# The values of self-attention as 2 by 2 blocks: seven half-width products for eight

## Chip, cores, metric

The kernel runs on one core of one Trainium2 chip. Time is device time in microseconds (us) of one execution; a kernel is run several times and the median is quoted. A second source is the profile: one execution recorded by the hardware profiler, with every engine instruction's start and duration. TensorE is called PE in it (PEld its weight loads), VectorE DVE, ScalarE ACT, GpSimd POOL, and the queue that issues most DMAs SP.

## What is computed

One decoder layer in fp32, on 8 sequences of 112 tokens with 512 features: causal self-attention with 16 heads of 128, cross-attention to 8 contexts of 375 tokens, and a mixture-of-experts feed-forward. Only the values of the first part concern the change:

```python
k = jnp.einsum('ihd,bpd->biph', W_K, x)
q = jnp.einsum('ihd,bpd->biph', W_Q, x)
v = jnp.einsum('ihd,bpd->biph', W_V, x)
...
attn = jax.nn.softmax(masked / jnp.sqrt(jnp.float32(d_head)), axis=-1)
z = jnp.einsum('biqp,biph->biqh', attn, v)
```

For a group of four heads, `v` is a product of 896 tokens by 512 features with a weight of 512 by 512.

## The kernel before

**Tokens.** The 896 tokens stand in seven tiles of 128. Tile t holds the 112 tokens of sequence t + 1 and, in its last 16 rows, a seventh of sequence 0. `xn1` is the normalised input, features on the partitions in four chunks of 128 and the 896 tokens along the free axis; HALF is 448 tokens.

**Groups.** Self-attention runs over four groups of four heads (`for g in range(NG)`). In each, PE makes the queries and keys, then the values with the first scores, then the weighted sums and the output projection (`project_o`, L340 to L351). One pass over a group takes about 108 us.

**Queries and keys.** `pair_of_heads` (L249 to L282) already makes them as 2 by 2 blocks in Winograd's form, seven products for eight. Tokens are halved (first and last 448), features are halved, and the two heads of a pair are the two column halves. The token sums `xc` are made once, by `token_sums`; the weight sums are made by POOL for each pair (L253 to L256, in tiles `wc` with three buffers). Products go to PSUM; DVE (L273, L277, L280 to L282), ACT (L271, L275) and POOL (L278, L279) add them up.

**Values.** `value(t)` (L335 to L343) makes a plain product for one tile: four chunks of features, each a matmul of 128 stationary columns (tokens) and 512 moving columns, summed in one PSUM tile; ACT copies it to `vals[t + 1]`, and SP moves its last 16 rows to the tile `vals[0]` of sequence 0. The calls stand between the scores: `softmax(b)` for the sequences 1, 0, 2, 3, 4, one value tile after each, then two more tiles. A matmul in fp32 is two records of PE in the profile, so a group has 56 records for its values.

**Softmax.** `softmax(b)` gives PE four small matmuls (L191) and then a chain: DVE adds the mask (L199), takes the maximum (L206) and subtracts it (L207), ACT takes the exponential (L208), DVE sums (L210) and inverts (L211), POOL multiplies (L212). Sequences 5 to 7 are done after the values, between `turn` (transposes, L218, copied by ACT at L220) and `weighted` (L226, evicted by DVE at L233).

**Order and buffers.** A scheduler puts each engine's instructions into one fixed order when the program is built, and each engine works through its own in order, waiting on semaphores. PSUM tiles of the values come from the pool `mm`, four buffers that are used in turn: a product needs the eviction of the one four before it. The weights of the next group are loaded by SP during the group, as soon as a buffer is free.

Of the kernel before, what the change touches and what calls it, by code (L numbers as in the profile page):

```python
# [27 lines left out]
HALF = NT // 2  # L28
H, DH = 16, 128
GH = 4  # L30
# [46 lines left out]
def decoder_layer(  # L77
    ctx: ExitStack, tc: tile.TileContext, x, ctxT, wqk, wv_all, wo, wx, wgate, wsgu, wsd, wegu, wed_a, wed_b, consts, out
):
    nc = tc.nc  # L80
# [7 lines left out]
    mm = ctx.enter_context(tc.tile_pool(name="mm", bufs=4, space=PSUM))  # L88
# [67 lines left out]
    def ln_apply(mv, rs, t, xnT):  # L156
        xn = ln_normed(mv, rs, t)
        pt = psum(mm, "ln_t")
        for c in range(ND):
            nc.tensor.transpose(pt[:, c * P : (c + 1) * P], xn[:, c * P : (c + 1) * P], ident)  # L160
        nc.scalar.copy(xnT[:, :, t * P : (t + 1) * P], pt.rearrange("p (c s) -> p c s", c=ND))


    xn1 = xnpool.tile([P, ND, NT], F32, tag="xnT", name="xn1")
    mv1 = ln_begin("1")

    def norm1(lo, hi):
        for t in range(lo, hi):
            ln_stats(mv1, t)
        return [ln_rstd(mv1, lo, hi)] * (hi - lo)  # L170
# [6 lines left out]
    with ExitStack() as sa:  # L177
        wvpool = sa.enter_context(tc.tile_pool(name="weights_vo", bufs=2))
        xcp = sa.enter_context(tc.tile_pool(name="x_sums", bufs=1))
        wcp = sa.enter_context(tc.tile_pool(name="w_sums", bufs=3))  # L180
        up = sa.enter_context(tc.tile_pool(name="part", bufs=2))
        qkp = sa.enter_context(tc.tile_pool(name="qk", bufs=1))
        vp = sa.enter_context(tc.tile_pool(name="v", bufs=TT))
# [100 lines left out]
        for g in range(NG):  # L284
            if g == 0:

                wq, wk = (wpool.tile([P, 4, 512], F32, tag="w", name=f"w{i}_0") for i in range(2))
                for h in range(GH):
                    for i, w in enumerate((wq, wk)):
                        nc.sync.dma_start(out=w[:, h, :], in_=wqk[i, g][:, h, :])  # L290
            else:
                wq, wk = (load_w(wpool, wqk[i, g], f"w{i}_{g}") for i in range(2))
            wv = load_w(wvpool, wv_all[g], f"w2_{g}")
            wog = wvpool.tile([P, 4, 512], F32, tag="w", name=f"wo_{g}")
            load = nc.sync.dma_start(out=wog, in_=wo[g])
            if g == 0:
                first_weights = load.ins
                with tc.issue_after(first_weights):
                    nc.sync.dma_start(out=gw, in_=wgate)
                    nc.sync.dma_start(  # L300
                        out=slots.rearrange("(j p) d -> p j d", p=P),
                        in_=zeros[:, None, :].to_broadcast([P, NS, D]),
                    )
            qT = qkp.tile([P, GH, NT], F32, tag="qT", name="qT")
            kT = qkp.tile([P, GH, NT], F32, tag="kT", name="kT")
            zT = zp.tile([P, GH, NT], F32, tag="zT", name="zT")
            for h in range(0, GH, 2):
                for w, dst, pool in ((wq, qT, mm), (wk, kT, sc)):
                    if g == 0 and h == 0 and dst is qT:

                        for half in range(2):
                            cols = bass.ds(half * HALF, HALF)
                            for i in range(2):
                                ps = psum(mm, "qk")
                                for c in range(ND):
                                    nc.tensor.matmul(
                                        ps[:, :HALF],
                                        w[:, i, c * P : (c + 1) * P],
                                        xn1[:, c, cols],
                                        start=(c == 0),  # L320
                                        stop=(c == ND - 1),
                                    )
                                nc.scalar.copy(dst[:, i, cols], ps[:, :HALF])
                            if half == 0:
                                rs1 = norm1(4, TT)
                                for t in range(4, TT):
                                    ln_apply(mv1, rs1[t - 4], t, xn1)
                                token_sums()
                        continue
                    pair_of_heads(w, h, dst, pool)  # L330
            soft, turned, vals = {}, {}, {}
            vals[0] = v0p.tile([S, GH * DH], F32, tag="v0", name="v0")

            def value(t):

                ps = psum(mm, "v")
                for c in range(ND):
                    nc.tensor.matmul(  # L338
                        ps, xn1[:, c, t * P : (t + 1) * P], wv[:, c, :], start=(c == 0), stop=(c == ND - 1)
                    )  # L340
                vals[t + 1] = vp.tile([P, GH * DH], F32, tag="v", name="v")
                nc.scalar.copy(vals[t + 1], ps)
                nc.sync.dma_start(out=vals[0][t * SP : (t + 1) * SP, :], in_=vals[t + 1][S:, :])  # L343

            def project_o(t):
                ps = psum(mm, "o")
                for h in range(GH):
                    nc.tensor.matmul(  # L348
                        ps,
                        zT[:, h, t * P : (t + 1) * P],  # L350
                        wog[:, h, :],  # L351
                        start=(h == 0),
                        stop=(h == GH - 1),
                    )
                nc.vector.tensor_tensor(xs[t], ps, xs[t], ALU.add)  # L355
                if g == NG - 1:
                    ln_stats(mv2, t)


            q0 = vp.tile([P, GH, S], F32, tag="q0", name="q0", bufs=1)  # L360
            nc.gpsimd.tensor_copy(like_seq(q0, 0), seq(qT, 0))
            for i, b in enumerate((1, 0, 2, 3, 4)):
                soft[b] = softmax(b, qT, kT, q0)
                value(i)
            for i in (5, 6):
                value(i)
            for b in (1, 0):
                turned[b] = turn(soft.pop(b))
            for b in range(1, B):
                if b + 4 < B:  # L370
                    soft[b + 4] = softmax(b + 4, qT, kT, q0)
                if b + 1 < B:
                    turned[b + 1] = turn(soft.pop(b + 1))
                weighted(b, turned.pop(b), vals.pop(b), zT)
                if b == 2:
                    weighted(0, turned.pop(0), vals.pop(0), zT)
                elif b > 2:
                    project_o(b - 3)
            project_o(TT - 2)
            project_o(TT - 1)  # L380
# [8 lines left out]
    with ExitStack() as xa:  # L389
# [14 lines left out]
        values = [v1p.tile([MC, NM, XH, VW], F32, name=f"v1_{i}") for i in range(2)]  # L404
# [49 lines left out]
        wt = [stp.tile([P, 2, 512], F32, name=f"wt{i}") for i in range(2)]  # L454
# [24 lines left out]
        def product(x, w):  # L479
            ps = psum(mm, "kv")  # L480
            for c in range(2):
                nc.tensor.matmul(ps[:MC, :], x[:, c, :], w[:, c, :], start=(c == 0), stop=(c == 1))  # L482
            return ps[:MC, :]
# [244 lines left out]
    with ExitStack() as ff:  # L728
# [37 lines left out]
        part = rp.tile([P, NT], F32, name="part")  # L766
# [124 lines left out]
        rows = []  # L891
# [282 lines left out]
```

## Time and profile before

| | us |
|---|---|
| median of 5 runs | 1019.46 (1017.88 to 1021.17) |
| the profiled execution | 1021.62 |
| its span (first to last engine instruction) | 1019.8 |
| PE busy | 997.1, 98% of the span |
| DVE, ACT, POOL busy | 401.4, 277.1, 246.8 |
| granted PE clock, mean | 0.996 |
| values, matmuls of the four groups (L338) | 224 records |

A busy time counts each moment once, even where matmuls overlap in the pipeline. The chain of waits follows the end of the program back, at each step to what released it; its pieces add up to the time. A stage table gives each engine's busy time in a stretch of the span.

### The profile page before, as it was taken

Reading aid. Unit: us, or ns where it says so; the run is one execution under the profiler, and the core shown is the slowest. Engines: PE = TensorE matmul, PEld = TensorE weight load, DVE = VectorE, ACT = ScalarE, POOL = GpSimd, SP = SyncE. Lnnn points to the kernel's source line nnn. Section 1 sums busy time; section 2 is a strip of 40 time slices with the busy share of each in tenths; the row PEclk is TensorE's granted clock in tenths of the full one; section 3 lists DMA queues with packets and bytes.
Section 4 is the critical chain, followed back from the end, with each engine's and each line's share of the span. In section 5 each row is a group of like instructions: output and inputs, shape, how many; then the busy total and the mean of one; then the engine's idle time right before and its main releaser. Section 6 shows DMA issues by size and latency. Waiting matters only on the chain.

```text
span 1019.8 us, 14761 instructions
## 1 busy us (share of the span) xinstructions
PE 997.1 (98%) x5732; PEld 530.8 (52%) x5732; DVE 401.4 (39%) x769; ACT 277.1 (27%) x522; POOL 246.8 (24%) x269
## 2 busy tenths in 40 slices
PE   5999999999999999999999999999999999999998
PEld 3556555554556455645455555555565544444433
DVE  3345224442345225545432434343424333333315
ACT  2122011210022012214354555445543111112200
POOL 3241034112511122122533213330205500000023
PEclk9999999999999999999999999998999999999999
DMA  9421012101101111000000100000209838777665
GB/s 348 190 86 48 0 42 84 50 1 42 61 30 43 42 41 47 5 1 0 31 31 2 31 31 32 2 31 2 83 2 369 298 93 276 233 232 235 214 194 168
DMA packets 31093, 95.66 MB, mean 94 GB/s; under 512 B 3888, under 2 KB 5808, under 8 KB 27440
## 3 DMA queue, kind: packets, MB, share of 16 engines
q1 hardware_dynamic: 25968, 82.11, 23.7%
q0 software_dynamic: 2320, 7.63, 2.3%
q10 hardware_dynamic: 2736, 4.98, 1.7%
q8 instruction: 46, 0.75, 0.3%
q14 instruction: 23, 0.19, 0.1%
HBM read 78.85 MB, written 14.94 MB: 92 GB/s over the span
## 4 chain that ended last, share of the span: by engine, by line
PE 90%; DVE 4%; issue 3%; POOL 1%; DMA 1%; ACT 1%; SPq 0%; DVEq 0%; POOLq 0%; ACTq 0%
PE qk L261 15%; PE o L348 9%; PE v L338 9%; PE kv L482 9%; PE gu L744 5%; PE xs L577 5%; PE gate L980 4%; PE y L1002 4%; PE up L980 4%; PE pv L602 4%; PE ys L1028 3%; PE k L423 3%; PE xv L423 3%; PE z L226 2%; PE s L191 2%
## 5 line engine op out<-in xcount | busy, mean ns | idle before, releaser
L585 ACT ACTIVATE e<-xs 125x448 f32<-125x448 f32 x192 | 88.6, 545 | 73.3 <-PE xs L577 73.2
L338 PE MATMUL v<-w,xn 128*128 128x512 f32 x224 | 100.4, 594 | 0.0
L348 PE MATMUL o<-wo,zT 128*128 128x512 f32 x224 | 99.8, 594 | 0.0
L261 PE MATMUL qk<-xc,wc 128*128 128x448 f32 x180 | 70.1, 539 | 0.0
L348 PEld LDWEIGHTS o<-wo,zT 128*128 128x128 f32 x224 | 41.0, 190 | 44.1 <-issue 44.0
L338 PEld LDWEIGHTS v<-w,xn 128*128 128x128 f32 x224 | 40.7, 190 | 42.1 <-issue 41.1
L212 POOL TENSOR_TENSOR s<-s,sm 112x448 f32<-112x448 f32 x32 | 30.1, 942 | 128.7 <-DVE sm L211 112.4
L1013 POOL DMA_INDIRECT got<-routed,at x14 | 14.9, 1066 | 172.6 <-DMA routed<-y 168.5
L980 PE MATMUL gate<-wex,xT 128*64 x144 | 55.3, 466 | 0.5 <-ACT xT L945 0.5
L744 PE MATMUL gu<-xn,sw 128*128 128x448 f32 x144 | 55.5, 541 | 0.0
L980 PE MATMUL up<-wex,xT 128*64 x144 | 54.3, 459 | 0.0
L577 PE MATMUL xs<-qT,kT 32*125 32x224 f32 x768 | 51.6, 378 | 1.5 <-DVE qT L540 1.5
L261 PEld LDWEIGHTS qk<-xc,wc 128*128 128x128 f32 x180 | 34.2, 190 | 33.5 <-issue 32.3
L930 DVE COPY xn<-wex 128x704 f32 x60 | 31.2, 525 | 51.5 <-PE up L980 51.5
L577 PEld LDWEIGHTS xs<-qT,kT 32*125 32x125 f32 x768 | 33.8, 184 | 32.7 <-issue 28.7
L261 PE MATMUL qk<-xn,w 128*128 128x448 f32 x120 | 50.2, 539 | 0.0
L1002 PE MATMUL y<-wd,hT 128*64 128x512 f32 (+1 forms) x216 | 49.5, 593 | 0.6 <-ACT y L1006 0.6
L980 PE MATMUL gate<-xn,xT 128*64 128x352 f32 x120 | 45.9, 464 | 0.0
L980 PE MATMUL up<-xn,xT 128*64 128x352 f32 x120 | 45.3, 459 | 0.0
L355 DVE TENSOR_TENSOR x<-o,x 128x512 f32<-128x512 f32 x28 | 19.3, 690 | 62.2 <-PE o L348 62.2
L271 ACT COPY p<-qk 128x448 f32<-128x448 f32 x15 | 8.0, 532 | 126.7 <-PE qk L261 126.7
L208 ACT ACTIVATE s<-s 112x448 f32<-112x448 f32 x32 | 18.5, 577 | 84.2 <-DVE s L207 78.9
(211 smaller groups left out, 1672.9 us busy)
## 6 DMA issues: line engine op xcount, KB each, us to landing
wd<-in_wed_a SPq DMA_DIRECT2D x27, 512.0 KB, 3.7
wex<-in_wegu SPq DMA_DIRECT2D x8, 1408.0 KB, 19.3
wd<-in_wed_b SPq DMA_DIRECT2D x36, 192.0 KB, 4.4
w<-in_wqk SPq DMA_DIRECT2D x6, 1024.0 KB, 4.9
ctx<-in_ctxT SPq DMA_DIRECT2D x8, 750.0 KB, 8.8
slots<-zeros SPq DMA_DIRECT2D x1, 4608.0 KB
wd<-in_wed_a SPq DMA_DIRECT2D x18, 256.0 KB, 4.2
routed<-y SPq DMA_DIRECT2D x18, 256.0 KB, 3.3
```

Source lines behind the costliest of these rows:

```text
L261: nc.tensor.matmul(ps[:, :HALF], wt[:, c * P : (c + 1) * P], x[:, c, :], start=(c == 0), stop=(c == 1))
L338: nc.tensor.matmul(ps, xn1[:, c, t * P : (t + 1) * P], wv[:, c, :], start=(c == 0), stop=(c == ND - 1))
L348: nc.tensor.matmul(ps, zT[:, h, t * P : (t + 1) * P], wog[:, h, :], start=(h == 0), stop=(h == GH - 1),)
L423: nc.tensor.matmul(ps[:MC, :], ctxs[b][:, c, m * MC : (m + 1) * MC], w[:, c, :], start=(c == 0), stop=(c == ND - 1),)
L482: nc.tensor.matmul(ps[:MC, :], x[:, c, :], w[:, c, :], start=(c == 0), stop=(c == 1))
L577: nc.tensor.matmul(strips[j][:MC, ci * 2 * S : (ci + 1) * 2 * S], keys[b][rows, 2 * cp + ci, m * MC : (m + 1) * MC], queries[b][rows, 2 * ...
L585: last_exp[(b, cp, m)] = nc.scalar.activation(e[:, :, j, :, :].rearrange("p c e s -> p c (e s)"), strips[j][:MC, : 4 * S].rearrange("p (c ...
L602: nc.tensor.matmul(ps[VW * j : VW * (j + 1), g * S : (g + 1) * S], v[:, m, 16 * cp + h, :], es[m][:, h // 8, (h % 8) // 2, h % 2, :], star ...
L744: nc.tensor.matmul(ps[:, :HALF], w[:, c, i % 2, k, :], xn3[:, c, cols], start=(c == 0), stop=(c == ND - 1))
L930: nc.vector.tensor_copy(second(j, c), wex[:, bass.ds(moved[j], 1), c, :].rearrange("p o f -> p (o f)"))
L980: nc.tensor.matmul(gu[k][n, :FF], xT[:, c, n], w, start=(c == 0), stop=(c == ND - 1))
L1002: nc.tensor.matmul(ps[n, :], hT[:fn, i, n], w[i][:fn], start=(i == 0), stop=(i == len(FCH) - 1))
```

## The change

The values of a group are made in two parts.

`values_left()` makes the first 64 tokens of tile 0 and the last 64 tokens of tile 3 plainly. For each chunk of features, two matmuls with 64 stationary columns and 512 moving columns stand next to each other as column tiles of the array: one writes the PSUM rows 0 to 63, the other the rows 64 to 127 of the same PSUM tile. ACT copies the two halves to `vals[1]` and `vals[4]`.

`values()` makes the rest in three rounds of 2 by 2 blocks. In round i the low tokens are the 128 from token 64 + 128 i on (half of one tile and half of the next), and the high tokens are 448 later, which is exactly tile 4 + i. The columns are halved to 256 (`wide`). The token sums `xc` of the queries and keys are used again; four weight sums (128 x 512 elements each) are new and are made by POOL in two tiles of the pool behind `wc`. Each round has seven products of two matmuls with 256 moving columns, and each product its own PSUM tile from `mm`. They are combined by DVE (two additions to `u2` and `u3`, one to the high tile, and four of 64 rows, `low`, which write the rows of one half tile from PSUM rows of the other half), by ACT (two copies) and by POOL (two additions).

The generator yields after every product; after each of the five early `softmax` calls four products are taken, and the last one after them. `values_left()` stands ahead of the first softmax. The copies of the last 16 rows of each tile (`tail`) are issued at the end of each round.

```diff
-            def value(t):
-                ps = psum(mm, "v")
-                for c in range(ND):
-                    nc.tensor.matmul(
-                        ps, xn1[:, c, t * P : (t + 1) * P], wv[:, c, :], start=(c == 0), stop=(c == ND - 1)
-                    )
-                vals[t + 1] = vp.tile([P, GH * DH], F32, tag="v", name="v")
-                nc.scalar.copy(vals[t + 1], ps)
-                nc.sync.dma_start(out=vals[0][t * SP : (t + 1) * SP, :], in_=vals[t + 1][S:, :])
+            def values_left():
+                ps = psum(mm, "v")
+                n = P // 2
+                for c in range(ND):
+                    for rows, lo in ((slice(0, n), 0), (slice(n, P), HALF)):
+                        nc.tensor.matmul(
+                            ps[rows, :], xn1[:, c, lo : lo + n], wv[:, c, :], start=(c == 0), stop=(c == ND - 1)
+                        )
+                nc.scalar.copy(vals[1][:n, :], ps[:n, :])
+                nc.scalar.copy(vals[4][n:, :], ps[n:, :])
+            wide = D // 2
+            b11, b12 = wv[:, 0:2, :wide], wv[:, 0:2, wide:]
+            b21, b22 = wv[:, 2:4, :wide], wv[:, 2:4, wide:]
...
+            nc.gpsimd.tensor_tensor(wt[0], b12, b11, ALU.subtract)
+            nc.gpsimd.tensor_tensor(wt[1], b22, wt[0], ALU.subtract)
+            nc.gpsimd.tensor_tensor(wt[2], b22, b12, ALU.subtract)
+            nc.gpsimd.tensor_tensor(wt[3], b21, wt[1], ALU.subtract)
+            def values():
+                n = P // 2
+                for i in range(3):
+                    lo = bass.ds(n + i * P, P)
+                    hi = bass.ds(HALF + n + i * P, P)
+                    high = vals[5 + i]
+                    def product(x, cols, w):
+                        ps = psum(mm, "v")
+                        for c in range(2):
+                            nc.tensor.matmul(ps[:, :wide], x[:, c, cols], w[:, c, :], start=(c == 0), stop=(c == 1))
+                        return ps[:, :wide]
...
+                    def low(cols, a, b):
+                        nc.vector.tensor_tensor(vals[1 + i][n:, cols], a[:n], b[:n], ALU.add)
+                        nc.vector.tensor_tensor(vals[2 + i][:n, cols], a[n:], b[n:], ALU.add)
+                    p1 = part("p1")
+                    nc.scalar.copy(p1, product(xn1[:, 0:2], lo, b11))
+                    yield
+                    u2 = part("u2")
+                    nc.vector.tensor_tensor(u2, product(xc[:, 1], lo, wt[1]), p1, ALU.add)
+                    yield
+                    p5 = part("p5")
+                    nc.scalar.copy(p5, product(xc[:, 0], lo, wt[0]))
+                    yield
+                    u3 = part("u3")
+                    nc.vector.tensor_tensor(u3, product(xc[:, 2], lo, wt[2]), u2, ALU.add)
+                    nc.gpsimd.tensor_tensor(high[:, wide:], p5, u3, ALU.add)
+                    nc.gpsimd.tensor_tensor(p5, p5, u2, ALU.add)
+                    yield
+                    low(slice(0, wide), product(xn1[:, 2:4], lo, b21), p1)
+                    yield
+                    nc.vector.tensor_tensor(high[:, :wide], product(xn1[:, 2:4], hi, wt[3]), u3, ALU.add)
+                    yield
+                    low(slice(wide, D), product(xc[:, 3], lo, b22), p5)
+                    tail(i)
+                    tail(4 + i)
+                    yield
+                tail(3)
...
-            for i, b in enumerate((1, 0, 2, 3, 4)):
+            values_left()
+            products = values()
+            for b in (1, 0, 2, 3, 4):
                 soft[b] = softmax(b, qT, kT, q0)
-                value(i)
-            for i in (5, 6):
-                value(i)
+                for _ in range(4):
+                    next(products)
+            for _ in products:
+                pass
```

In the built program a group has 50 matmuls for the values where it had 28: 8 of 64 stationary and 512 moving columns, and 42 of 128 stationary and 256 moving columns. The order of everything after self-attention is unchanged.

More of the change, by code (lines that the diff above doesn't have):

```diff
@@ L332, in decoder_layer, with tail @@
             vals[0] = v0p.tile([S, GH * DH], F32, tag="v0", name="v0")
-            def value(t):
+            for t in range(TT):
+                vals[t + 1] = vp.tile([P, GH * DH], F32, tag="v", name="v")
+            def tail(t):
+                nc.sync.dma_start(out=vals[0][t * SP : (t + 1) * SP, :], in_=vals[t + 1][S:, :])
+            def values_left():
                 ps = psum(mm, "v")
+                n = P // 2
                 for c in range(ND):
-                    nc.tensor.matmul(
-                        ps, xn1[:, c, t * P : (t + 1) * P], wv[:, c, :], start=(c == 0), stop=(c == ND - 1)
-                    )
-                vals[t + 1] = vp.tile([P, GH * DH], F32, tag="v", name="v")
-                nc.scalar.copy(vals[t + 1], ps)
-                nc.sync.dma_start(out=vals[0][t * SP : (t + 1) * SP, :], in_=vals[t + 1][S:, :])
+                    for rows, lo in ((slice(0, n), 0), (slice(n, P), HALF)):
[4 more added lines that the diff above has]
+                nc.scalar.copy(vals[4][n:, :], ps[n:, :])
@@ new lines, in decoder_layer @@
+            wide = D // 2
+            b11, b12 = wv[:, 0:2, :wide], wv[:, 0:2, wide:]
+            b21, b22 = wv[:, 2:4, :wide], wv[:, 2:4, wide:]
+            wt = [
+                w[:, k : k + 2, :]
+                for w in (wcp.tile([P, 4, wide], F32, tag="wc", name=f"wvs{i}") for i in range(2))
+                for k in (0, 2)
+            ]
+            nc.gpsimd.tensor_tensor(wt[0], b12, b11, ALU.subtract)
+            nc.gpsimd.tensor_tensor(wt[1], b22, wt[0], ALU.subtract)
+            nc.gpsimd.tensor_tensor(wt[2], b22, b12, ALU.subtract)
@@ new lines, in decoder_layer, with part @@
+            nc.gpsimd.tensor_tensor(wt[3], b21, wt[1], ALU.subtract)
[10 more added lines that the diff above has]
+                        return ps[:, :wide]
+                    def part(name):
+                        return up.tile([P, HALF], F32, tag=name, name=name)[:, :wide]
+                    def low(cols, a, b):
[24 more added lines that the diff above has]
+                tail(3)
```

## The prediction

> **What bounds the kernel now.** First the page: busy times, and the chain that ended last.
>
> ```profile
> PE 997.1 (98%) x5732; PEld 530.8 (52%) x5732; DVE 401.4 (39%) x769; ACT 277.1 (27%) x522; POOL 246.8 (24%) x269
> PE 90%; DVE 4%; issue 3%; POOL 1%; DMA 1%; ACT 1%; SPq 0%; DVEq 0%; POOLq 0%; ACTq 0%
> PE qk L261 15%; PE o L348 9%; PE v L338 9%; PE kv L482 9%; PE gu L744 5%; PE xs L577 5%; PE gate L980 4%; PE y L1002 4%; PE up L980 4%; PE pv L602 4%; PE ys L1028 3%; PE k L423 3%; PE xv L423 3%; PE z L226 2%; PE s L191 2%
> ```
>
> PE is the bound, and the values are 9% of the chain: what PE saves there is time, unless another engine takes its place. So next, the stage table of the second group: the values with their scores, and the stretch behind them.
>
> ```profile
> 169.30:197.69 28.39, 28.39 (x98) 14.68 (x97) 13.93 (x26) 6.39 (x11) 7.62 (x10) 1.00 0.14 45
> 197.69:206.40 8.71, 8.09 (x78) 7.94 (x76) 6.71 (x14) 4.10 (x8) 0.94 (x2) 1.00 0.37 124
> ```
>
> The columns are span, then busy PE, PEld, DVE, ACT, POOL. In the values DVE is half free. Behind them PE has its only gap of the group, 0.6 us, and DVE is busy 6.7 of 8.7. The chain of waits there, in order of time:
>
> ```profile
> 186.76 0.79 PE s L191 x8
> 187.54 10.31 PE v L338 x24
> ...
> 199.45 0.64 DVE s L199
> ...
> 200.11 0.62 DVE mx L206
> 200.73 0.62 DVE zT L233
> 201.35 0.53 DVE s L207
> 201.89 0.54 DVE s L199
> ...
> 203.38 1.12 PE z L226 x8
> ...
> 206.56 3.45 PE o L348 x8
> ```
>
> Here the chain leaves PE: the softmax of sequences 5 and 6 and the evictions zT stand on one DVE queue, and it starts 1.76 us after the last value product (199.45 less 197.69). What makes DVE later at this point delays PE one for one.
>
> **The PE term.** The chain gives pitches, which the mean durations (pipelined) do not. A group's values take 24.12 us on it (0.87 + 2.59 + three times 3.45 + 10.31), so 0.431 for each of 56 records of 512 columns. A record of 256 columns with 128 stationary ones isn't in this trace. Half of 0.431 is 0.215. The line through the 448-column products of the same chain (112 in 42.09 us, 0.376) and the 112-column z (8 in 0.89, 0.111) gives 0.225; the line through 448 and 512 columns gives 0.211. I take 0.215, since the two nearest widths run at 0.84 ns a column, and keep the others as ends. 84 records make 18.06 us. The half tiles are like the expert products, which run as pairs of 64 columns:
>
> ```profile
> 854.02 0.74 PE gate L980 x4
> 854.76 0.59 PE up L980 x4
> ...
> 856.54 2.58 PE y L1002 x12
> ```
>
> y has 512 moving columns: 12 records in 2.58 us, 0.215 each because two run side by side. 16 records make 3.44. The first gate row, just after 128-column transposes, is 0.15 longer than its neighbours; the timeline puts 0.09 to 0.10 of that on each change between the two tilings. Two changes a group make 0.2. Sum: 24.12 - 3.44 - 18.06 - 0.2 = 2.42 us a group, 9.7 over four.
>
> **The DVE term.** Rows, by shape:
>
> ```profile
> L207 DVE TENSOR_TENSOR s<-s,mx 112x448 f32<-112x448 f32 x32 | 19.9, 623 | 0.8
> L632 DVE TENSOR_TENSOR t<-o_t,r 128x256 f32<-128x256 f32 x14 | 5.9, 424 | 0.4
> L500 POOL TENSOR_TENSOR v<-p,kraw 125x512 f32<-125x512 f32 x7 | 8.9, 1265 | 2.7 <-ACT p L499 2.7
> L530 DVE TENSOR_TENSOR q<-q,qss 128x512 f32<-128x512 f32 x7 | 5.4, 778 | 0.4
> ```
>
> L632 reads PSUM and SBUF at 256 columns, as all 21 new additions of a group do: 21 x 0.424 = 8.9 us. Those of 64 rows have no row; fewer rows need not be cheaper. From below 0.277 (the 96x128 copy at L995), from above 0.62 (a 448-wide addition); I take 0.424, the same columns. The five softmaxes stay, 4 x 0.62 + 0.18 each, 13.3 in all. Together 22.2. From the end of the first scores (3.44 + 0.1 + 0.79 = 4.3 us into the stage) to the last product (3.44 + 0.2 + 18.06 + 5 x 0.79 = 25.65) there are 21.3 us. That looks too little, but DVE operations that don't wait on each other overlap: 201.35 to 201.89 in the chain is a step of 0.54 for an operation of 0.62. At some 0.08 for 25 of them 2 us go, leaving 20.2, and about 1 us for waits on the exponential. In the built order additions now stand between L207 and L210, where before DVE idled 0.5 us each (16.5 us for 32). And PE may run four products (3.4 us) ahead, through the four buffers of mm. So inside the stage I charge nothing.
>
> Behind it: the last addition needs the sum p5, made by POOL. In POOL's built order four weight sums of the next group's second pair (0.73 each, L253 to L256) stand ahead of the two additions of the last round, and they wait until the third product of that round has read its weights, since the tile is shared. That product ends four products, 3.4 us, before the last. 4 x 0.73 + 2 x 0.73 = 4.4 us: p5 is there 1.0 us after the last product, two additions of 0.42 follow, and L199 starts at about 1.9 to 2.1 instead of 1.76: 0.3 late. After that POOL still makes sums for the third pair, beside L207. In this trace an operation with both inputs in SBUF that met POOL took 1294 ns instead of 691 (L530), and one of L553 1168 instead of 686, by as much as POOL had left. L207 now meets POOL; before it did once in 32. I charge half a weight sum, 0.4. So 0.7 us in each of three groups; the last has no next group, 0.2. Stall: 2.3 us.
>
> [...]
>
> **What lies beside.** The four weight sums (1.27 each by L500, 5.1 a group) lie in POOL's queue in the queries and keys, ahead of the p5 sums of the last pair; POOL is busy 19.6 of 70.5 us from the projection to the values, so they cost nothing. Without that cover the second product would wait up to 2.5. The half tiles stand ahead of the first scores and hide the last key evictions, behind that queue. ACT has 2 copies of 0.585 and 6 of about 0.37 for 7 of 0.585: less. SP has the same seven row copies; the last goes out about 2.5 us after the products instead of 0.8, behind the next value weights in both versions (issue at 197.89, 5.0 us to land), and z of sequence 0 (203.38) waits for that landing before and after: nothing.
>
> **The sum.** 9.7 - 2.3 = 7.4 us. The profiled execution was 1021.62, which would become 1014.2; it lies 2.2 above the median of 1019.46, so the median becomes **1012.1**. What a measurement here can tell from no change is 0.2%, 2 us. Own range 1009 to 1016: no stall at all gives 1009.8, and with cheaper half-row additions a little less; the 0.225 pitch costs 84 x 4 x 0.010 = 3.4, 1015.5.
>
> **Rivals.**
> *DVE fills the stage and hands its lag on.* If the five waits on the exponential remain (2.5 us) and the overlap is half (1 us), DVE needs 23.7 for 21.3 and starts softmax 5 2.4 + 0.8 us after the products, 1.5 late; with 0.4 for L207 the stall is 1.9 of 2.42. Net 0.5 a group: 1017.4, with 1016 to 1020. For it: the arithmetic above is within 1 us. Against: the evictions now fill the waits.
> *DVE becomes the bound: slower.* If additions that read one half of the partitions and write the other take a 448-wide operation's time, and the full ones too, 21 x 0.2 = 4.1 us are added a group; 4.1 + 0.6 - 2.42 = 2.3 lost, four times: 1028.6. It decides from 0.424 + (2.42 - 0.6) / 21 = 0.51 us an addition. Against: L632 at 0.424 with the same sources; for: no row has 64 rows moved across.
> *It doesn't save PE work.* 50 matmuls replace 28, but the built order shows the widths halved; only a pitch of 0.244 would undo it, above both lines. Under 2 in 100, counted with the second.
>
> **Chances.** Forecast 0.70, lag 0.17, slower 0.13. About half of the lag's case lies above 1017.4. Faster by over 0.2%: 0.77; within: 0.11; slower: 0.12. For 8 in 10 the range takes in most of the lag: 1008.8 to 1018.8.
>
> **What would show it.** In the chain of the profile after: value products at 0.43 us for a pair of records, two tiling changes of 0.1; a group 1.7 us shorter in the first three and over 2 in the last; L199 of sequence 5 starting 1.9 to 2.3 us after the last product; the 64-row additions at 0.42; L207 above 0.63 where it meets L253 to L256. Wrong if PE idles inside the values, if a 256-column record steps by over 0.225, or if additions exceed 0.5.

## The result and the profile after

The changed kernel takes 1019.7 us (median of 51 runs, 1015.5 to 1023.4); the kernel before, measured beside it, takes 1017.97 us. The ratio is 1.0015, with a 95% interval of 1.0009 to 1.0022. The forecast was 1012.1, with a range that ended at 1018.8. So nothing was gained, and a little was lost. The profiled execution took 1018.11 us, with a span of 1016.3.

The page after: busy times, and the shares of the chain that ended last.

```profile
PE 986.5 (97%) x5908; PEld 553.6 (54%) x5908; DVE 436.0 (43%) x853; ACT 273.9 (27%) x526; POOL 284.4 (28%) x309
PE 82%; DVE 10%; issue 4%; ACT 1%; POOL 1%; DMA 1%; SPq 0%; DVEq 0%; POOLq 0%; ACTq 0%
```

PE is busy 10.6 us less than before (997.1). Some 3.4 of that, and as much of the 3.5 by which the span is shorter, is a stretch of 6.83 us at half clock, from 702 us on, that the execution of before had and this one had not. In the chain DVE has gone from 4% to 10%. The stage table of the second group says where (span, then busy PE, PEld, DVE, ACT, POOL):

```profile
169.70:195.50 25.80, 25.80 (x141) 21.00 (x141) 19.65 (x41) 6.16 (x13) 10.13 (x14) 1.00 0.16 48
195.50:206.46 10.96, 8.67 (x78) 7.98 (x76) 9.83 (x21) 3.60 (x7) 7.09 (x10) 1.00 0.31 102
```

From the first record of the stage to the last, PE needs 25.80 us where it needed 28.05 (169.65 to 197.69; the row of before began 0.35 earlier, with the end of the keys). It does not idle inside. Behind the values, to the first output projection, it takes 10.96 where it took 8.71, with 2.3 us idle. What was saved is handed back to 0.1 us. The same table for all groups, read from the records of PE:

| group | values before | after | behind them before | after | net |
|---|---|---|---|---|---|
| 1 | 28.05 | 25.80 | 8.50 | 11.27 | +0.5 |
| 2 | 28.05 | 25.81 | 8.70 | 10.95 | 0.0 |
| 3 | 28.05 | 25.81 | 8.71 | 10.96 | 0.0 |
| 4 | 28.05 | 25.81 | 8.54 | 9.08 | -1.7 |

Only the last group, which makes no weight sums for a next one, keeps most of it. The chain of waits of the same stretch, in order of time:

```profile
193.58 1.05 DVE s L207
194.65 0.58 ACT s L208
195.26 0.62 DVE sm L210
...
197.03 0.44 DVE v L405
197.46 0.74 POOL p L401
198.22 0.42 DVE v L386
198.64 0.03 issue
198.67 0.43 DVE v L387
199.10 0.03 issue
199.13 0.64 DVE s L199
199.79 0.62 DVE mx L206
200.41 0.53 DVE zT L233
200.94 1.36 DVE s L207
...
206.46 3.70 PE o L416 x8
```

Nearly all of the chain is on DVE. Softmax 5 starts (L199) 3.63 us after the last product (199.13 less 195.50), where before it was 1.76. Two things in it are not DVE's own: it waits for POOL's second p5 addition (L401), and its subtractions of the maximum (L207), of softmax 4 and of softmax 5, take 1.05 and 1.44 us (the chain's 1.36 is a part of that) where they took 0.62. POOL's timeline shows what stood ahead of that addition:

```profile
192.52 0.93 POOL L212 TENSOR_TENSOR s<-s,sm 112x448 f32<-112x448 f32 x1 [3.80 <-DVE sm L211]
193.41 0.72 POOL L253 TENSOR_TENSOR wc<-w 128x256 f32<-128x256 f32 x1
194.10 1.11 POOL L255 TENSOR_TENSOR wc<-w 128x256 f32<-128x256 f32 x1
195.16 0.72 POOL L254 TENSOR_TENSOR wc<-w,wc 128x256 f32<-128x256 f32 x1
195.97 0.73 POOL L256 TENSOR_TENSOR wc<-w,wc 128x256 f32<-128x256 f32 x1
196.65 0.73 POOL L400 TENSOR_TENSOR v<-p,u 128x256 f32<-128x256 f32 x1
197.46 0.73 POOL L401 TENSOR_TENSOR p<-p,u 128x256 f32<-128x256 f32 x1
```

The four weight sums of the next group began at 193.41, behind a scaling (L212) that itself had waited 3.8 us for DVE. One of them (L255) lay beside L207 and was drawn out as well.

### The profile page after: what moved, and what is told of

Its sections match the earlier page's. It is cut to its first block, busy times and chain, and to the rows that moved or that the text cites. A ratio compares the mean times of both kernels' runs of the same rounds, so it can differ in the third digit from the quotient of the medians.

```text
span 1016.3 us, 15302 instructions
## 1 busy us (share of the span) xinstructions
PE 986.5 (97%) x5908; PEld 553.6 (54%) x5908; DVE 436.0 (43%) x853; ACT 273.9 (27%) x526; POOL 284.4 (28%) x309
## 4 chain that ended last, share of the span: by engine, by line
PE 82%; DVE 10%; issue 4%; ACT 1%; POOL 1%; DMA 1%; SPq 0%; DVEq 0%; POOLq 0%; ACTq 0%
PE qk L261 16%; PE o L416 10%; PE kv L553 9%; PE gu L815 5%; PE xs L648 5%; PE gate L1051 4%; PE y L1073 4%; PE up L1051 4%; PE pv L673 4%; PE ys L1099 3%; PE k L494 3%; PE xv L494 3%; PE v L378 2%; DVE s L207 2%; PE z L226 2%
## 5 line engine op out<-in xcount | busy, mean ns | idle before, releaser
L212 POOL TENSOR_TENSOR s<-s,sm 112x448 f32<-112x448 f32 x32 | 29.8, 932 | 79.6 <-DVE sm L211 75.5
L483 POOL TENSOR_TENSOR sq<-kraw 125x512 f32<-125x512 f32 x24 | 25.1, 1047 | 59.4 <-ACT kraw L517 37.4
L553 PE MATMUL kv<-wx,ctx 128*125 128x512 f32 x84 | 40.4, 603 | 0.0
L484 DVE TENSOR_REDUCE kss<-sq 125x32 f32<-125x512 f32 x24 | 16.5, 686 | 55.5 <-POOL sq L483 55.5
```

## The experiments

The theory: PE's saving is real, and what takes it back is DVE leaving the stage late, for three reasons that add up: its own work, p5 late in POOL's queue, and L207 held up by POOL. The rivals: something else sets the 107.8 us of a group, or the clock. In some of the edited kernels line numbers are two or three higher (L209 is L207 there).

### The causes one by one

Four kernels on one chip, against 1018.09 for the kernel before. First the changed kernel again.

> The changed kernel once more, as the base of the three beside it. Lag theory (the 2.3 us that TensorE saves in a group's value stage is handed back because VectorE leaves the stage late): 1019 to 1020 us with the same granted clock as the kernel before in most runs. Clock theory (the new idle gaps of TensorE bring windows of half clock): the runs of the changed kernel show a lower mean clock than those of the kernel before, by 0.002 to 0.003, which is 2 to 3 us of the time.

Measured: 1019.91 us, ratio 1.0021 (1.0004 to 1.0038). That is in the range of the lag theory; the clock theory's sign is there as well: the mean clock of the runs was 0.996 against 0.998, and below 0.9975 in 10 of 12, against 14 of 35 of the kernel before. The clock is taken up below.

GpSimd's sums out of the way:

```diff
-            nc.gpsimd.tensor_tensor(s, s, sm[:, :, None].to_broadcast([S, GH, S]), ALU.mult)
+            scaled[b] = nc.gpsimd.tensor_tensor(s, s, sm[:, :, None].to_broadcast([S, GH, S]), ALU.mult).ins
...
-            nc.gpsimd.tensor_tensor(t[:, 0], b12, b11, ALU.subtract)
...
+            with tc.issue_after(scaled[B - 1]) if scaled else ExitStack():
+                nc.gpsimd.tensor_tensor(t[:, 0], b12, b11, ALU.subtract)
...
```

> GpSimd's sums of the next group's query and key weights are queued behind the scaling of sequence 7's softmax, so they no longer stand ahead of the additions of p5 at the end of the value stage, and no longer lie beside VectorE's subtraction of the maximum. GpSimd theory (p5 late by 1.7 us and the blocked subtractions, 1.04 and 1.44 us for 0.63, make the lag): the last addition comes about 0.8 us earlier, the two subtractions 0.4 and 0.8 us shorter, 1.5 to 2 us a group in the first three groups, so 1013.5 to 1015.5 us. VectorE theory (the stage holds 24.8 us of VectorE's work without a gap, and GpSimd only waits for it): under 0.7 us a group, 1017.5 to 1019.5 us.

Measured: 1015.06 us, ratio 0.9964 (0.9945 to 0.9983). The stretch behind the values, second group:

```profile
193.70:202.65 8.95, 8.24 (x78) 7.92 (x76) 8.59 (x20) 3.71 (x7) 2.54 (x3) 1.00 0.36 125
```

10.96 became 8.95: 2.0 us of the 2.25 are back, in each of the first three groups. p5 is there 0.7 us after the last product, softmax 5 starts at 2.45 instead of 3.63, and L209 takes 0.62 again. So of the lateness 1.18 us were POOL's. The other part, 2.45 against 1.76, is DVE's own: in this run its last three additions and L201 (L199) follow each other without a wait.

```profile
194.78 0.42 DVE L408 TENSOR_TENSOR v<-v,u 128x256 f32<-128x256 f32 x1
195.24 0.42 DVE L389 TENSOR_TENSOR v<-v,p 64x256 f32<-64x256 f32 x1
195.69 0.43 DVE L390 TENSOR_TENSOR v<-v,p 64x256 f32<-64x256 f32 x1
196.15 0.62 DVE L201 TENSOR_TENSOR s<-s,cst 112x448 f32<-112x448 f32 x1
```

Six additions fewer on DVE:

```diff
-                nc.scalar.copy(vals[1][:n, :], ps[:n, :])
+                nc.scalar.copy(vals[4][:n, :], ps[:n, :])
...
-                        nc.vector.tensor_tensor(vals[1 + i][n:, cols], a[:n], b[:n], ALU.add)
-                        nc.vector.tensor_tensor(vals[2 + i][:n, cols], a[n:], b[n:], ALU.add)
+                        nc.vector.tensor_tensor(vals[1 + i][:, cols], a, b, ALU.add)
```

> The two 64-row additions of each low product are made as one addition of 128 rows into one tile (the rows of the values are then put 64 places off, and the upper half of tile 0's values is written by it; the output is not the reference's). Six additions of 0.43 us fewer in a group, 2.6 us of VectorE's 24.8. VectorE theory: the start of softmax 5 moves from 3.6 us behind the last product to 1.8 at most, TensorE's gaps behind the stage shrink by 1.5 to 2.2 us in each of the first three groups and by about 1 in the last: 1011.5 to 1014.5 us. GpSimd theory: the last addition still waits for p5 at 2.7 us, so 0.5 us a group, 1017 to 1018.5 us.

Measured: 1013.4 us, ratio 0.9957 (0.9938 to 0.9975). Both theories were too simple here: the stretch behind took 9.84 us in the second group, half-way between, while the median fell by 6.5. Of the 6.5, 3.8 are in the four stretches of the profiles (1.3, 1.1, 0.8 without the half-clock window that the third had, and 0.6), and 1.2 in a copy at the end of the program that has nothing to do with the values (see "The sum" below). DVE's timeline of the second group:

```profile
191.64 0.39 DVE L404 TENSOR_TENSOR v<-v,u 128x256 f32<-128x256 f32 x1
193.65 0.42 DVE L386 TENSOR_TENSOR v<-v,p 128x256 f32<-128x256 f32 x1 [1.61 <-POOL p L400]
193.99 0.61 DVE L199 TENSOR_TENSOR s<-s,cst 112x448 f32<-112x448 f32 x1
```

DVE is done with its own work when the last product ends (192.05) and then stands still for 1.6 us, waiting for p5. The additions and the queue are both binding; whichever is taken away shows the other.

The products spread out:

```diff
-                for _ in range(4):
+                for _ in range(3):
                     next(products)
-            for _ in products:
-                pass
...
+                for _ in range({1: 3, 2: 9}.get(b, 0)):
+                    next(products, None)
                 weighted(b, turned.pop(b), vals.pop(b), zT)
-                if b == 2:
+                if b == 4:
...
-                elif b > 2:
-                    project_o(b - 3)
+                elif b > 4:
+                    project_o(b - 5)
...
```

> The same instructions in another order: six of the 21 products are issued behind the value stage, between the turns and the softmaxes of sequences 5 and 6, and the product of sequence 0 and the output projections two steps later. Lag theory (TensorE's saving is real and only lacks cover behind the stage): the products fill the gaps that VectorE's lag opens, 2 to 2.3 us a group, 1010 to 1013 us. If the time is lost elsewhere (clock, or a bound of the whole group's 107.8 us on another engine): 1018 to 1021 us as without it.

Measured: 1019.1 us, ratio 1.0013 (0.9995 to 1.003). The expectation failed. A group got shorter by 0.8 us only (first projections at 102.68, 209.70 and 316.73). The six products bring their additions with them, onto the same DVE queue, between softmax 5 and 6. Work that loads the late engine is no cover for it. Its mean clock was 0.993 in 6 of the 12 runs, so the run does not tell the theories apart by its time. How its remaining gaps come about was not taken further.

### Cover, and which part of POOL

DVE's timeline of the changed kernel shows it idle for 3.86 us at the start of the stage, while PE makes the half tiles, which need nothing of it. The next run moves them to the end.

```diff
+                tail(3)
...
-                tail(3)
...
-            values_left()
             products = values()
...
             for _ in products:
                 pass
+            values_left()
```

> The two half tiles are multiplied behind the 21 products instead of ahead of them (sequence 0's rows of tile 3 follow them); nothing else differs from the changed kernel. VectorE has nothing to do for 3.9 us at the start of the value stage (its first row, at 174.36 us of the profiled execution, is ended by the scores) and is 3.6 us behind at its end. Lag theory: it starts 3.6 us earlier, and both its lag and the late p5 lie beside the half tiles' 3.6 us of TensorE, so first output projection 8.7 us or less behind the last value matmul, about 2.3 us a group: 1009 to 1012 us. If something else than VectorE and GpSimd set the 107.8 us of a group: 1018 to 1020 us.

Measured: 1013.04 us, ratio 0.9951 (0.9932 to 0.997). The mechanism held, the size did not: 9.49 us behind the values, not 8.7. Softmax 5 now waits 1.29 us for PE's scores, not PE for softmax 5. PE has one wait left, 1.35 us at the product of sequence 0.

The next run has the half tiles last and POOL's sums late as well. It is the "best version" of what follows.

> The same, and with GpSimd's sums of the next group's weights behind sequence 7's softmax. If the half tiles' place already covers p5 and only the blocked subtractions are left: 0.5 to 1 us a group better than with the half tiles last alone, 1007 to 1010 us. If GpSimd's sums behind the stage cost nothing once the lag is gone: the same as that run within 1 us.

Measured: 1009.28 us, ratio 0.991 (0.9888 to 0.9932). Stage tables of the second group, with the half tiles last and then with the sums late as well:

```profile
194.51:204.00 9.49, 8.14 (x78) 7.99 (x77) 7.54 (x16) 4.68 (x9) 5.04 (x7) 1.00 0.38 121
```

```profile
193.32:201.93 8.61, 8.14 (x79) 7.99 (x77) 6.62 (x14) 4.67 (x9) 0.93 (x1) 1.00 0.40 130
```

The stretch is as short as it was before the change, and the value stage keeps its 25.9 us: a group takes 105.5 us where it took 107.7.

Which of POOL's two effects counts? The sums were put behind the last p5 addition only, still ahead of the late softmaxes:

> GpSimd's sums of the next group's weights are queued behind the last addition of p5 in the value stage, so ahead of the scaling of sequences 5 to 7: the queue ahead of p5 is as short as with the sums behind sequence 7's softmax, but the sums now lie beside VectorE's subtractions of softmax 5 and 6. Queue theory (p5 ready late is what cost the time): as with the sums behind the softmaxes, 0.995 to 0.997 of the kernel before. Blocking theory (the subtractions drawn out from 0.63 to 1.04 and 1.44 us, and GpSimd's own sums from 0.73 to 1.11 us, are the larger part): half of that gain is gone, 0.998 to 1.000.

Measured: 1017.1 us, ratio 0.9995 (0.9977 to 1.0013); 10.5 us behind the values in the second and third group, where late sums gave 8.95. p5 is early, and of the 2.0 us that late sums gave in a stretch 0.4 is left; by the medians about half is. DVE's timeline and then POOL's, at softmax 5:

```profile
199.56 0.61 DVE L235 COPY zT<-z 128x448 f32<-128x448 f32 x1
200.09 1.98 DVE L209 TENSOR_TENSOR s<-s,mx 112x448 f32<-112x448 f32 x1
202.00 0.61 DVE L201 TENSOR_TENSOR s<-s,cst 112x448 f32<-112x448 f32 x1
```

```profile
200.19 0.72 POOL L259 TENSOR_TENSOR wc<-w,wc 128x256 f32<-128x256 f32 x1
200.88 0.71 POOL L257 TENSOR_TENSOR wc<-w,wc 128x256 f32<-128x256 f32 x1
201.56 1.11 POOL L258 TENSOR_TENSOR wc<-w 128x256 f32<-128x256 f32 x1
```

The subtraction, 0.62 us by itself, takes 1.98: it comes to its end only when two sums are through, and the next sum is drawn out to 1.11 in turn. This is the blocking theory's answer; in the stretch it is stronger than the theory said. The eviction of zT just ahead, which reads PSUM, is not drawn out: 0.61 us beside a scaling of POOL (0.93 from 199.30).

Late sums in the kernel before:

> The kernel before, with GpSimd's sums of the next group's weights behind sequence 7's softmax, to see how much of the better order's gain is the order's alone. Theory of the lag: the plain values put no additions on VectorE and no p5 behind those sums, so only the blocked subtractions of a group are shortened: 0 to 0.4 us a group, 0.9985 to 1.000 of the kernel before. If the order pays by itself: 0.996 or less.

Measured: 1018.25 us, ratio 1.0007 (0.9989 to 1.0024). The later sums alone give nothing to the kernel before: the order is worth something only with the new additions in the way.

### The best version, and what no longer counts

> The best version so far once more (half tiles last, GpSimd's sums of the next group behind sequence 7's softmax), since it had only six runs, as the base of the two beside it: 1008 to 1011 us, 0.989 to 0.993 of the kernel before, and a clock of 0.998 or more in most runs. If the six were a lucky draw of the clock: 1012 us or more with clocks of 0.995 to 0.997 in half of the runs.

Measured: 1009.29 us, ratio 0.9906 (0.9885 to 0.9928). The first six runs were no luck.

> The best version with the two 64-row additions of each low product made as one of 128 rows (rows of the values put 64 places off; the output is not the reference's). Theory that VectorE's extra work counts only where nothing covers it: its lag is gone already (2.4 us idle ahead of softmax 5), so 2.6 us a group less of its work gives nothing, within 1 us of the best version. If VectorE's work itself sets the time of a group: 1.5 to 2 us a group less, 1001 to 1004 us.

Measured: 1008.73 us, ratio 0.9908 (0.9888 to 0.9929). The same 2.6 us of DVE's work that took 3.8 us out of the stretches of the changed kernel are worth 0.6 here, which is within the scatter of five and six runs. Covered work has no price.

> The best version with the product of sequence 0 and the output projections one step later. In the best version the last wait of a group behind the values is 0.5 us at sequence 0's product, whose accumulation buffer VectorE frees when it has read the scores of softmax 6. If one step later covers that: 0.3 to 0.5 us a group, 1 to 2 us in all. If the wait only moves to sequence 3's product or the first projection: the same within 1 us.

Measured: 1010.31 us, ratio 0.9911 (0.9892 to 0.9931): no gain. The wait moved, as in the second theory though to another place, to a gap of 0.55 us at the transposes of sequence 7, and a group takes 105.5 us as before. That run left open what the wait at sequence 0 was for. The profile of the best version names VectorE, which had long been done; that of its second run names the copy of the rows at one of the two waits left (0.3 us).

### The wait at sequence 0

The times point to a copy. In the best version, SyncE's timeline and the copies' landings:

```profile
191.88 1.14 SPq L344 DMA_DIRECT2D v<-v  x2
193.43 0.33 SPq L122 DMA_DIRECT2D w<-in_wv  x1
194.65 0.51 SPq L344 DMA_DIRECT2D v<-v  x1
DMA to landing us min/median/max: 1.9/1.9/4.1
```

The last copy of sequence 0's rows goes out at 194.65, behind 1 MB of weights, takes 4.1 us instead of 1.9, lands at about 198.75, and the product starts at 198.91. With the half tiles last alone, where the late p5 held up SyncE's queue as well, it went out at 195.84, took 5.0, and the product started at 200.99. The test puts the load behind the copy:

```diff
-            wv = load_w(wvpool, wv_all[g], f"w2_{g}")
+            with tc.issue_after(tails[-1]) if tails else ExitStack():
+                wv = load_w(wvpool, wv_all[g], f"w2_{g}")
```

> The best version (half tiles last, GpSimd's sums behind sequence 7's softmax) with the load of the next group's value weights queued behind the last copy of sequence 0's rows on SyncE's queue. In the best version that copy goes out at 194.65 us, 1.2 us behind the 1 MB load, takes 4.1 us to land instead of 1.9, and the product of sequence 0 starts at 198.91 after 0.47 us of idle TensorE. Theory that this landing is the last wait of a group: the copy lands 2 us earlier, 0.3 to 0.5 us a group, 1 to 2 us in all: 1007.5 to 1008.5 us, 0.989 to 0.990 of the kernel before. Rival, VectorE's reading of the scores of softmax 6: no gain, within 0.7 us.

Measured: 1007.82 us, ratio 0.9906 (0.9891 to 0.9922). The stretch behind the values in the second group:

```profile
190.64:199.17 8.53, 8.53 (x82) 8.33 (x81) 6.54 (x14) 4.67 (x9) 0.93 (x1) 1.00 0.41 131
```

All copies land in 1.9 us, and PE's 0.47 us of idle time are gone: 8.53 busy of 8.53. PE now works through a whole group without a stop, and a group takes 104.95 us. That is where the gain shows; the ratio to the kernel before, measured beside it, is the 0.9906 that the best version's second run had.

> The kernel before with the same single edit: the load of the next group's value weights behind the last copy of sequence 0's rows. Its only gap of a group, 0.6 us, is at the same product. Theory of the landing: 0.5 to 0.6 us in each of three groups, 1.5 to 2 us in all, 0.998 of the kernel before. Rival: no change.

Measured: 1015.12 us, ratio 0.9987 (0.9978 to 0.9995). PE's idle time behind the values fell from 0.62 to 0.05 us. So the kernel before had this wait too, and the fair comparison is between these two: 1007.82 against 1015.12, 7.3 us by medians of 5 and 12 runs for the blocks in the values once the order suits them. By the profiles a group takes 104.95 us against 107.16: 2.21, all of the 2.24 that PE saves.

### The clock

> The changed kernel, one look for the place of its half-clock windows. Gap theory: windows of about 3.4 us begin within some 2 us of the first output projection of a group, right behind TensorE's gaps of 1.1 to 1.8 us at the end of the value stage, none or up to three of them in one execution; the time is about 1016.5 us plus 1.7 us for each. Rival: the windows lie in the later stages, near 700 us, as in the profile of the kernel before, and have nothing to do with the gaps.

> The same once more. Gap theory: again windows of 3.4 us behind TensorE's gaps in groups one to three; rival: near 700 us.

> The kernel with six products behind the value stage, whose runs show the low clock most often (10 of 12) and whose TensorE gaps of 0.8 to 1.0 us stand just ahead of the output projections. Gap theory: windows of 3.4 us that begin at the output projections of groups one to three. Rival: near 700 us.

> The kernel before, without those gaps (its largest idle stretch behind the values is 0.6 us). Gap theory: no window at the output projections; a window near 700 us in about a third of the executions. Rival: windows at the output projections here too.

Measured: 1015.61, 1023.29, 1018.34 and 1017.58 us. The profile of the first has no half-clock window ahead of the last few microseconds of the span; the second has one of 3.41 us from 207.29 and one of 6.83 us from 702.22; the third has 6.83 us from 95.1 and 3.41 us from 207.7; the fourth has none. The first repeat of the changed kernel had windows from 204.92 and from 314.14. In the changed kernel all three in the attention begin within 0.6 us of a first output projection. In the spread order they follow its idle stretches of 1.8 us, ahead of the projections and not at them as expected. The kernel with six additions fewer had one as well, from 306.46 in its third group, behind an idle stretch of 2.13 us. The window table of that repeat, three neighbouring stretches around the first:

```profile
201.00:204.90 3.90, 2.23 (x16) 1.60 (x15) 3.77 (x9) 0.99 (x2) 1.29 (x2) 1.00 0.00 0
204.90:208.30 3.40, 3.40 (x6) 1.34 (x5) 2.48 (x5) 0.58 (x1) 0.57 (x1) 0.50 0.00 0
208.30:212.00 3.70, 3.70 (x19) 2.37 (x18) 1.31 (x2) 0.53 (x1) 0.93 (x1) 1.00 0.00 0
```

The third figure from the end is the granted clock: 0.50 for 3.4 us, a cost of 1.7 us as an estimate from the two. The same 3.4 us just ahead of the first projection, in the first of these four executions (no window followed), and the emptiest stretch of the kernel before, ahead of the window at 702 of its profile:

```profile
200.90:204.30 3.40, 1.73 (x15) 1.33 (x12) 3.29 (x9) 1.00 (x2) 0.93 (x1) 1.00 0.00 0
```

```profile
697.49:700.90 3.41, 1.81 (x14) 1.26 (x13) 3.31 (x6) 2.34 (x5) 0.68 (x1) 1.00 0.00 0
202.99:206.40 3.41, 3.02 (x29) 3.06 (x29) 3.23 (x9) 1.11 (x2) 0.94 (x2) 1.00 0.00 0
```

Both theories held a part. A stretch of 3.41 us with PE busy for about half of it can bring a window, and need not: the first execution had 1.73 and no window. The kernel before and the changed kernel each have one such place near 700 us (1.81 in both profiles), and one near 500 us (1.95 and 1.94) that no half clock followed in either. The change adds three, at the end of the values of the first three groups (1.7, 1.7 and 2.1 of 3.41 by the records), where the kernel before was busy for 2.8 to 3.0. The windows of one execution lie on a grid: in the profile of before the window is 6.83 us long, and the full clock lasted 682.67 us ahead of it and 310.61 behind it, 200 and 91 times 3.413, which is half of 6.83. Of the other distances 314.14 less 204.92 is 32 of them, and 702.22 less 207.29 is 145. The grid lies elsewhere in each execution: counted back from the half clock at the end of its span, that of the first profile of the changed kernel has a mark at 202.50, where the first repeat has one at 204.92 and the second execution here one at 207.29. That this decides whether a gap is hit is the author's reading. Cut along its own grid, that profile holds 1.84 of PE's work there (202.50 to 205.91) and not 1.73 (203.05 to 206.46). The stretches that a half-clock window followed held 1.74 (203.90 to 207.30 of the second execution), 1.75 and 2.10 (201.48 to 204.89, and 310.60 to 314.05, 3.45 long, of the first repeat) and 1.81 (698.62 to 702.03 of before). None followed the 1.84, nor 1.93 and 2.15 (from 697.44 and 311.73 of the same profile), nor 1.95 (from 504.06 of before). So between 1.8 and 2.1 it went both ways. In the 1.81 of before half a window of work did not prevent the half clock, though the longest idle stretch in it was 1.07 us.

The runs agree in number: the mean clock was below 0.9975 in 47 of 65 runs of the changed kernel, in 28 of 92 of the kernel before, and in none of 22 of the three orders without the gaps (the best version twice, sequence 0 later, copy first). The figure 0.9975 divides them only roughly: the kernel with six additions fewer has a window in its profile at a mean clock of 0.998. Single kernels scatter: with late sums it was 7 of 12, with one addition per low product on top of the best version 2 of 6, in the kernel before with the copy first 0 of 12. Behind the values of the second group the first of these has 0.71 us of idle PE (8.24 busy of 8.95), and the last 0.05. Why the place near 700 is hit so unevenly stays open: from 690 to 710 us the granted clock was 0.83 in the profiles of before and of the second execution here, and 1.00 in the first repeat.

## Why the prediction was wrong

**The PE term was right.** 2.42 us a group were forecast and 2.24 measured (28.05 less 25.81). Four records of 256 columns step by 0.86, the half tiles take 3.58, and PE does not idle in the stage, as said.

**"So inside the stage I charge nothing" is the step that failed.** The 22.2 us of DVE's work were right: in DVE's timeline of the run with late sums the 46 operations of the second group's stage add up to 22.1, the additions of 64 rows at 0.42 each. What failed is the 2 us taken off for overlap. Only ten of them overlap the next, by 0.08, 0.8 in all. The others are followed at a distance of 0.03 (the last additions start at 194.78, 195.24 and 195.69, steps of 0.45 for operations of 0.42), which adds 1.0, and three waits for the exponential (0.31 each) and one for scores (0.36) add 1.3. So DVE needs 23.6 us from its first instruction to its last, in a window of 21.15 between the first scores (172.55) and the last product (193.70). It is 2.45 us late even with nothing in its way. The rival called lag had this sum (23.7 us, 2.4 late), though from other terms: 2.5 for waits and 1 off for overlap. The forecast chose the cheaper reading of the overlap.

**"p5 is there 1.0 us after the last product" failed as well.** It came after 2.7. The four sums were in the count, but the scaling ahead of them in POOL's queue was not. It waits for DVE, so the sums started 1.3 us later than the weights allowed, and one of them took 1.11 instead of 0.73, beside L207 (193.58 to 194.62). A lag on DVE fed itself through POOL and came back.

**"Half a weight sum, 0.4" for L207 was too small.** In the second group it lost 0.43 inside the stage, which was not charged, and 0.82 behind it. Over the kernel its mean went from 623 to 744 ns, 3.9 us in 32 operations:

```profile
L207 DVE TENSOR_TENSOR s<-s,mx 112x448 f32<-112x448 f32 x32 | 23.8, 744 | 0.4
```

In the run with the sums in the middle it is 790. The prediction took half a sum, since no row of the trace before showed L207 losing anything; by the runs it can lose two (1.98 for 0.62). The additions fed from PSUM kept their 0.42 beside POOL (196.57, 197.03 and 198.22 in DVE's timeline of the changed kernel).

**The sum.** Stalls of 0.7 in three groups and 0.2 in the last were forecast; 2.8, 2.25, 2.25 and 0.54 were measured. In the second group 1.87 of it is the later start of softmax 5 (3.63 less 1.76), and 0.38 what follows it. Saved 9.0, handed back 7.8. The queries and keys of the later groups take 0.1 to 0.2 us longer, so that from the start of the first values to the last projection some 0.8 us are won in the profile. The end of the program loses 1.2 again: the last copy of the output lands 2.93 us after its issue instead of 1.77, in all four profiles of the changed kernel (2.75 to 3.01) and in none of the four of the kernel before and its variants (1.76 or 1.77). What draws it out is not shown. Without its half-clock stretch the execution of before has the same span (1016.4 for 1016.3). The rest of the 1.7 us between the medians fits the half-clock windows: over all runs the mean clock is 0.9966 against 0.9987, which is some 2 us at most, as an estimate from these two, since part of it lies in the last microseconds, where PE has nothing to do. The forecast also started from a median of five runs; that of 94 is 1.5 lower (1017.97), and 7.4 off it is 1010.6.

**"Waits for that landing before and after: nothing"** was right for the change, but the wait itself was worth 0.5 us in each of three groups and easy to remove.

**The rivals.** The lag was the right one, at 0.17: DVE is late by its own work, as it said. Its 1.9 for a stall of 2.25 was in part luck. It put softmax 5 at 3.2 us behind the products by adding 0.8 for two additions that the 22.2 already held, where the run with late sums shows 2.45; the 1.18 that POOL adds to that it left out. "DVE becomes the bound" was wrong: additions stayed below 0.5. Of the signs named in advance, the 0.43 pairs, the 64-row additions and the drawn-out L207 came true, and the start of softmax 5 told the error at once: 3.63 where 1.9 to 2.3 stood.

## What to carry to other kernels

When work moves from the bound engine to one that looks half free, compare its work in that stage with the stage's length to the tenth, take nothing off for overlap that the same pair of instructions has not shown, and follow each shared queue to what its instructions wait for. Then look for stretches of the bound engine that ask nothing of the loaded one (here the half tiles) and put them where the lag comes out; that, and moving POOL's sums by ten microseconds, turned no gain into almost 9 us. A gap is also paid a second time if the clock drops behind it, as in the first repeat (0.50 for 3.4 us).

## What the runs showed of the hardware

DVE's subtraction L207, with both inputs in SBUF, and POOL's weight sums held each other up in both directions: 0.62 became 1.04 and 1.44 in the changed kernel and 1.98 with the sums in the middle, and POOL's 0.73 became 1.11; with the sums late it took 0.62. Additions with one input in PSUM stayed at 0.42 beside POOL. An addition of 64 rows took 0.42, as one of 128 did. A 32 KB copy landed in 1.9 us, and in 4.1 and 5.0 where it went out 1.2 and 0.6 us behind a load of 1 MB on the same queue. Half-clock windows of 3.41 and 6.83 us followed stretches of 3.4 us in which PE was busy for 1.74 to 2.10 us, on a grid of 3.413 us.
